# A 32x32-square transpose route through VectorE, DRAM and GpSimd in an attention-and-graph kernel

## The chip, the cores and the metric

The kernel runs on one core of one Trainium2 chip. The metric is device time in microseconds (us), lower is better. The kernel before takes 2595.5 us (median of three runs, 2594.34 to 2596.72).

## The reference

The input x has shape (16, 1024, 256): 16 batches of 1024 nodes with 256 channels. adj is 1024 x 1024. Everything is float32.

```
# layer 0, per batch
fea  = x^T                                    # (C, N)
c    = mean over channels of x                # (N,)
A    = 2*| |sigmoid(c_m - c_n) - 0.5| - 0.5 |,  symmetrised
g    = relu((fea @ (adj * A)) * para)         # (C, N)  -> queries, 4 heads of 64
k, v = x @ kv_w
out  = softmax(q k^T * scale) v               # 4 heads, concatenated to (N, C)
x1   = layernorm(x + out)
# layer 1
agg  = A_hat @ x1                             # A_hat: normalised adjacency
h    = relu(batchnorm(agg @ W1^T + b1))
y    = batchnorm(h @ W2^T + b2)
out  = layernorm(x1 + y)
```

The change touches layer 0 only, in two places: x is needed transposed (channels on partitions) for the keys and values, and the attention output, which comes out transposed (head and channel on partitions, 512 nodes along the row), has to be turned back before it is scaled by the reciprocal of the softmax denominator and added to x.

## The kernel before

Layer 0 takes the span from 0 to about 1725 us, layer 1 the rest. In layer 0 the attention of batch b and the preparation of batch b+1 are interleaved. The order on TensorE, VectorE and ScalarE is written out by hand; each of these engines executes its list in that order, so an instruction that waits holds everything behind it on its engine. SyncE (which issues most DMAs) and GpSimd also work through a list in order, but that list is put together by the scheduling layer from the program and the tile pools.

A batch has 32 *units*: 2 pairs of heads (`pr`) x 2 halves of the queries (`qh`) x 8 key blocks of 128 (`m`). A unit is

- `scores` (L926): TensorE makes 128 keys x (2 heads x 512 queries) in a PSUM tile `ps` (2 buffers),
- the exponential (L931): ScalarE, `ps` -> `p` in SBUF (pool `pp`, 4 buffers),
- `outputs` (L947): TensorE accumulates `po` over the 8 key blocks,
- `sums` (L955, L957): VectorE adds the `p` tiles up in `acc`, for the denominators. A `p` buffer is free again when both `outputs` and `sums` have read it.

Units go in bursts of two, 16 bursts (u = 0 to 15) a batch. In burst u TensorE does the scores of units 2u and 2u+1, and then the outputs of the two units before. So the exponential of the fifth unit of a batch, the first of burst u = 2, needs the `p` buffer of the first, which the VectorE addition L955 of units 0 and 1 releases.

When the 8 key blocks of one (pr, qh) are done, ScalarE (L964) and VectorE (L965) leave the unnormalised output in `oT` (128 x 512); k counts these tiles, 4 a batch, 64 in all. When both halves of a pair are done, `normalise` makes the denominators: TensorE (L977) into `den`, ScalarE (L983) to `drow`, SyncE writes 4 rows to DRAM (L985) and reads them back in columns (L990, `dcol`, 4 DMAs with 4-byte pieces).

`residual` (four times a batch) then takes VectorE's reciprocal of `dcol` (L998), 4 TensorE transposes of `oT` (L1004, `poT`), a VectorE product of `poT` with the reciprocals (L1008, `o`) and GpSimd's addition to x (L1013). All four of a batch are run in burst u = 0 of the next batch, between the projections `values` (L879) and `keys` (L866) of the batch after; these share the PSUM tiles `pt`, `ps`, `den` of the pool `t` (2 buffers). In u = 4 follow the layernorm statistics of that batch (L614, VectorE), which need all four additions, and 8 pairs of graph products (`graph_mm`, L829, first half of the channels). In u = 8 the second half of them is done, and around and between them the next-but-one batch begins: `begin` sums the channels (L774), writes the means to DRAM (L781) and reads them back on all partitions (L783, `crow`), and `transpose_x` makes 16 TensorE transposes of x (L790, `pxT`), copied to SBUF by VectorE and ScalarE (L794). `crow` is what ScalarE needs for the graph weights (`weights_abs` L810, `weights_tanh` L815; then `weights_adj` L819 on VectorE), the list `side`: 24 steps, 10 of them in bursts u = 9 to 15, the other 14 in u = 0 of the next batch.

For the first two batches the same steps run in a stretch of their own ahead of the bursts; in the last batch the residuals of batch 14 run in u = 2 and u = 5 and the first two of batch 15 in u = 13, the last two at the end.

## Time and profile before

| what | value |
|---|---|
| median of three runs | 2595.5 us |
| lowest, highest | 2594.34, 2596.72 us |
| span of the profiled execution, first to last instruction | 2592.7 us |
| TensorE busy | 2544.9 us, 98% |
| VectorE busy | 1573.9 us, 61% |
| ScalarE busy | 1214.5 us, 47% |
| GpSimd busy | 358.9 us, 14% |
| DMA | 140624 packets, 168.98 MB |
| one batch of layer 0, for example 1221.68 to 1326.09 | 104.41 us |

How to read it: the profile is one execution. The page gives its span and no other time for it; the runs' times are some us above the span. Times in timelines are us from the span's start. Busy is time in instructions, not counting the issuing of DMAs. "Idle before, releaser" is time in which an engine stood still ahead of an instruction, and what it was seen to wait for. A row of the timeline may merge several instructions in sequence (x4), and neighbouring rows overlap by some hundredths [...]. The chain of waits follows the last instruction back through what released it.

### The profile page before, as it was taken

The page shows a single profiled execution, that of the slowest core. Times are in us where ns is not written, and L with a number is a line of the kernel's source. Part 1 is how long each engine was busy: PE and PEld are TensorE (multiplying, and loading weights), DVE is VectorE, ACT ScalarE, POOL GpSimd, SP SyncE. Part 2 cuts the span into 40 slices and gives each one's busy share as a digit, 9 for nine tenths or more (in the row PEclk, how much of TensorE's full clock was granted, in tenths as well). Part 3 has the DMA queues.
Part 4 walks back from the last instruction along what each step waited for, and adds up shares of the span by engine and source line. Part 5 has one row for each costly group of instructions (what it writes and reads, how often), then busy time and mean ns, then how long its engine had stood idle before and what let it go on. Part 6 is the DMA issues. An engine that isn't in the chain of part 4 may idle for free.

```text
span 2592.7 us, 32521 instructions
## 1 busy us (share of the span) xinstructions
PE 2544.9 (98%) x13118; PEld 1119.8 (43%) x13118; DVE 1573.9 (61%) x2082; ACT 1214.5 (47%) x1499; POOL 358.9 (14%) x424
## 2 busy tenths in 40 slices
PE   9999999999999999999999999999999999999997
PEld 5443443434444444344344444344444444444455
DVE  5365655655646556566465575676556555568568
ACT  6375564655656646656466474521011100144458
POOL 0010100101101011011010110242112221010026
PEclk9999999999999999999999999999999999999999
DMA  4001101011011010110110101022122212255549
GB/s 146 1 10 42 33 10 42 2 42 34 10 42 34 9 42 1 42 33 10 42 31 12 38 5 50 10 82 92 71 86 92 97 65 98 81 195 176 189 168 345
DMA packets 140624, 168.98 MB, mean 65 GB/s; under 512 B 87089, under 2 KB 120369, under 8 KB 132017
## 3 DMA queue, kind: packets, MB, share of 16 engines
q1 hardware_dynamic: 135104, 115.95, 14.8%
q0 software_dynamic: 4832, 50.34, 4.7%
q8 instruction: 105, 1.72, 0.3%
q10 hardware_dynamic: 528, 0.52, 0.1%
q14 instruction: 55, 0.44, 0.1%
HBM read 99.36 MB, written 67.44 MB: 64 GB/s over the span
## 4 chain that ended last, share of the span: by engine, by line
PE 86%; DVE 9%; ACT 3%; issue 1%; DMA 0%; POOL 0%; SPq 0%; DVEq 0%; POOLq 0%; ACTq 0%
PE ps L926 16%; PE pg L829 16%; PE po L947 16%; PE pv L879 5%; PE b_agg L1366 4%; PE c_agg L1366 4%; PE pk L866 3%; PE po L1648 3%; PE a_agg L1366 2%; PE b_h L1398 2%; PE b_o L1574 2%; PE c_h L1398 2%; PE c_o L1574 1%; PE pxT L790 1%; PE a_h L1398 1%
## 5 line engine op out<-in xcount | busy, mean ns | idle before, releaser
L931 ACT ACTIVATE p<-ps 128x1024 f32<-128x1024 f32 x512 | 496.7, 1023 | 185.7 <-PE ps L926 156.1
L957 DVE TENSOR_TENSOR acc<-acc,p 128x1024 f32<-128x1024 f32 x384 | 485.7, 1265 | 122.8 <-ACT p L931 94.3
L926 PE MATMUL ps<-qT,kT 64*64 64x512 f32 x4096 | 491.0, 592 | 0.7 <-DVE qT L838 0.3
L947 PE MATMUL po<-p,v 64*64 64x512 f32 x4096 | 488.3, 589 | 0.8 <-ACT p L931 0.8
L829 PE MATMUL pg<-wg,x 128*128 128x512 f32 x960 | 420.9, 594 | 0.0
L1013 POOL TENSOR_TENSOR x<-x,o 128x512 f32<-128x512 f32 x64 | 122.2, 1909 | 1165.6 <-DVE o L1008 1165.6
L947 PEld LDWEIGHTS po<-p,v 64*64 64x64 f32 x4096 | 160.1, 133 | 281.0 <-issue 270.3
L829 PEld LDWEIGHTS pg<-wg,x 128*128 128x128 f32 x960 | 179.2, 190 | 221.3 <-issue 208.3
L926 PEld LDWEIGHTS ps<-qT,kT 64*64 64x64 f32 x4096 | 152.2, 133 | 281.3 <-issue 249.6
L838 DVE SCALAR_TENSOR_TENSOR qT<-pg,para_s 128x1024 f32<-128x1024 f32 (+1 forms) x34 | 39.2, 1161 | 236.1 <-PE pg L829 235.0
L819 DVE SCALAR_TENSOR_TENSOR wg<-wg,adj_s 128x1024 f32<-128x1024 f32 x128 | 162.2, 1279 | 21.7 <-ACT wg L815 21.7
L810 ACT ACTIVATE wg<-crow,ccol 128x1024 f32<-128x1024 f32 x128 | 147.1, 1150 | 8.2 <-DMA crow<-c 8.2
L815 ACT ACTIVATE wg<-wg 128x1024 f32<-128x1024 f32 x128 | 136.1, 1064 | 1.7
L879 PE MATMUL pv<-kvw_s,xT 128*128 128x256 f32 x512 | 126.8, 391 | 6.7 <-ACT kT L870 6.7
L965 DVE TENSOR_TENSOR oT<-po,oT 128x512 f32<-128x512 f32 x64 | 44.2, 691 | 145.6 <-ACT oT L964 145.6
L866 PE MATMUL pk<-xT,kvw_s 128*128 128x512 f32 x256 | 121.9, 598 | 3.3 <-ACT v L884 3.3
L624 ACT ACTIVATE x<-x,nm_l,rs_l 128x256 f32<-128x256 f32 x128 | 64.8, 588 | 110.2 <-POOL nm_l L620 110.2
L841 ACT ACTIVATE qT<-qT 128x1024 f32<-128x1024 f32 (+1 forms) x34 | 34.1, 1007 | 174.7 <-DVE qT L838 174.7
L879 PEld LDWEIGHTS pv<-kvw_s,xT 128*128 128x128 f32 x512 | 92.8, 190 | 50.1 <-ACT kT L870 25.1
L1366 PE MATMUL a_agg<-ahT,x1l 128*128 128x512 f32 x240 | 108.1, 593 | 0.7 <-ACT agg L1146 0.7
L1366 PE MATMUL b_agg<-aT,x1S 128*128 128x512 f32 x240 | 107.9, 592 | 0.0
L650 ACT COPY p_agg<-a_agg 128x512 f32<-128x512 f32 x15 | 8.8, 585 | 183.4 <-PE a_agg L1366 183.4
(204 smaller groups left out, 2933.1 us busy)
## 6 DMA issues: line engine op xcount, KB each, us to landing
h<-hw POOLq DMA_DIRECT2D x16, 2048.0 KB, 6.9
hl<-h SPq DMA_DIRECT2D x32, 1024.0 KB
x<-x POOLq DMA_DIRECT2D x16, 1024.0 KB, 4.2
x1l<-x SPq DMA_DIRECT2D x16, 1024.0 KB
xf<-x SPq DMA_DIRECT2D x16, 1024.0 KB
x<-in_x_dram SPq DMA_DIRECT2D x15, 1024.0 KB
out_dram<-o SPq DMA_DIRECT2D x12, 1024.0 KB
crow<-c SPq DMA_DIRECT2D x15, 512.0 KB
```

The lines of the kernel that those rows point to most:

```text
L810: nc.scalar.activation(w, s["crow"], AF.Abs, bias=s["ccol"][:, n : n + 1])
L815: nc.scalar.activation(w, w, AF.Tanh, scale=0.5)
L819: nc.vector.scalar_tensor_tensor(w, w, 1.0, adj_s[:, n, :], op0=ALU.subtract, op1=ALU.mult)
L829: nc.tensor.matmul(s["pg"][:, hs], xt[:, n, c * P : (c + 1) * P], s["wg", n][:, hs], start=(n == 0), stop=(n == NCH - 1),)
L866: nc.tensor.matmul(ps, kvw_s[:, c, kc * P : (kc + 1) * P], s["xT"][:, c, hs], start=(c == 0), stop=(c == CC - 1),)
L879: nc.tensor.matmul(pt[:, j * C : (j + 1) * C], s["xT"][:, c, n * P : (n + 1) * P], kvw_s[:, c, C : 2 * C], start=(c == 0), stop=(c == CC - 1),
L926: nc.tensor.matmul(ps[kh * D : (kh + 1) * D, hd * HALF : (hd + 1) * HALF], kT[r, pr, ks], qT[r, pr, qh * HALF : (qh + 1) * HALF], start=Tr ...
L931: nc.scalar.activation(p, ps, AF.Exp)
L947: nc.tensor.matmul(g["po"][kh][hd * D : (hd + 1) * D, :], s["v"][r, m, h * D : (h + 1) * D], p[r, hd * HALF : (hd + 1) * HALF], start=(m = ...
L957: nc.vector.tensor_add(g["acc"], g["acc"], p)
L1366: nc.tensor.matmul(ps, left, right, start=(start and i == 0), stop=(i == NCH // 2 - 1), skip_group_check=True,)
L1398: nc.tensor.matmul(ps, left, right, start=start, stop=True, skip_group_check=True)
```

## The change

For batches 2 to 15, x is loaded from DRAM a second time in 32x32 squares (`load_squares`: 4 DMAs of 1024 pieces of 128 bytes for each half of the channels, into a tile `xS` with one buffer), so that VectorE's transpose of 32x32 squares gives the transposed x in one instruction per half (`transpose_squares`, 128 x 1024). The first half is loaded in u = 5 of the program and transposed in u = 8, the second is loaded when the first has been transposed, and transposed in u = 11. The 16 TensorE transposes and 4 copies per batch go.

For 62 of the 64 attention outputs (all but the last pair of the last batch), `squares_to_rows` follows directly on `oT`: VectorE transposes the squares of `oT` into `oS`, SyncE writes `oS` to DRAM, and 4 SyncE DMAs of 512 pieces of 128 bytes bring it back as rows into a tile `o`, which comes from the pool `rdp` with one buffer. `residual` keeps VectorE's reciprocal; GpSimd multiplies `o` with it and adds the product to x. The TensorE transposes and VectorE's product go. The pool of `oT` has 2 buffers in place of 4.

The order of `side` changes: 10 steps in u = 0, 2 in u = 1, 2 in u = 2.

```diff
+    o_d = [
+        dram.tile([NQ, SQ, HALF // SQ, SQ], F32, tag=f"o_{g}", name=f"o_{g}")
+        for g in range(2 * B * H // 2)
+    ]
...
-        tc.tile_pool(name="op", bufs=4) as op,
+        tc.tile_pool(name="op", bufs=2) as op,
+        tc.tile_pool(name="xsp", bufs=1) as xsp,
...
+        def load_squares(b, c):
+            xs = st[b]["xS", c] = xsp.tile([P, N // SQ, SQ], F32, tag="xS", name=f"xS_{b}_{c}")
+            src = x[b].rearrange("(j k) (c q i) -> c q k j i", k=SQ, q=NQ, i=SQ)
+            for q in range(NQ):
+                nc.sync.dma_start(xs[q * SQ : (q + 1) * SQ], src[c, q])
...
+            def transpose_squares(c):
+                if c == 0:
+                    s["xT"] = xTp.tile([P, CC, N], F32, tag="xT", name=f"xT_{b}")
+                nc.vector.transpose(
+                    s["xT"][:, c, :], s["xS", c].rearrange("p j i -> p (j i)")
+                )
+                if c == 0:
+                    load_squares(b, 1)
...
-            for i in range(2 * CC):
-                first.append((transpose_x, (i // 2, i % 2) if b else (i % 2, i // 2)))
+            if b < 2:
+                for i in range(2 * CC):
+                    first.append((transpose_x, (i // 2, i % 2) if b else (i % 2, i // 2)))
+            else:
+                first += [(transpose_squares, (c,)) for c in range(CC)]
...
                 nc.vector.tensor_add(g["oT"], g["po"][1], g["oT"])
+                if (b, pr) != (B - 1, PAIRS - 1):
+                    squares_to_rows(b, pr, qh)
...
+        def squares_to_rows(b, pr, qh):
+            g = G[b, pr, qh]
+            k = (b * PAIRS + pr) * 2 + qh
+            oS = op.tile([P, HALF], F32, tag="oS", name=f"oS_{k}")
+            nc.vector.transpose(oS, g["oT"])
+            nc.sync.dma_start(o_d[k].rearrange("q i j d -> (q i) (j d)"), oS)
+            g["o"] = rdp.tile([P, 4, NQ, SQ], F32, tag="o", name=f"o_{k}")
+            src = o_d[k].rearrange("q i (n m) d -> m i n q d", m=NQ)
+            for m in range(NQ):
+                nc.sync.dma_start(g["o"][m * SQ : (m + 1) * SQ], src[m])
...
             nc.vector.reciprocal(r_all[:, k], g["col"])
-            if (b, pr) == (B - 1, PAIRS - 1):
-                pt = tile_s(f"poT_{k}")[:, H0]
-            else:
-                pt = tile_t(f"poT_{k}")
+            r = r_all[:, k].unsqueeze(3).to_broadcast([P, 4, 2, D])
+            xs = s["x"][:, 4 * qh : 4 * qh + 4, pr * P : (pr + 1) * P]
+            if (b, pr) != (B - 1, PAIRS - 1):
+                o = g["o"].rearrange("p n q d -> p n (q d)")
+                oh = o.rearrange("p n (h d) -> p n h d", d=D)
+                nc.gpsimd.tensor_tensor(oh, oh, r, ALU.mult)
+                nc.gpsimd.tensor_tensor(xs, xs, o, ALU.add)
+                return
...
                 if u == 5 and b + 2 < B:
                     load_x(b + 2)
+                    load_squares(b + 2, 0)
...
                         if b:
                             run(steps, 1)
-                            run(side, 2)
+                            if i < 5:
+                                run(side, 2)
...
-                    run(side, 99)
                     run(full, 1)
+                elif u < 4:
+                    run(side, 2 if u < 3 else 99)
...
                 elif u == 8:
-                    run(next_first, 3)
-                    for n in range(NCH):
-                        run(steps, 1)
-                        if n == 3:
-                            run(next_first, 2)
+                    run(next_first, 2)
+                    run(steps, NCH)
                     run(sums, 1)
                 elif u > 8:
+                    if u == 11:
+                        run(next_first, 1)
                     run(next_side, 2 - u % 2)
```

More of the change, by code (lines that the diff above doesn't have):

```diff
@@ L573, in fast_path @@
     h_d = [dram.tile([P, HC, N], F32, tag=f"h_{b}", name=f"h_{b}") for b in range(B)]
+    SQ = 32
+    NQ = P // SQ
+    o_d = [
+        dram.tile([NQ, SQ, HALF // SQ, SQ], F32, tag=f"o_{g}", name=f"o_{g}")
+        for g in range(2 * B * H // 2)
+    ]
     ident = const.tile([P, P], F32, name="ident")
@@ L998, in residual @@
             nc.vector.reciprocal(r_all[:, k], g["col"])
-            if (b, pr) == (B - 1, PAIRS - 1):
-                pt = tile_s(f"poT_{k}")[:, H0]
-            else:
-                pt = tile_t(f"poT_{k}")
+            r = r_all[:, k].unsqueeze(3).to_broadcast([P, 4, 2, D])
[6 more added lines that the diff above has]
+                return
+            pt = tile_s(f"poT_{k}")[:, H0]
             for j in range(4):
@@ L1008, in residual @@
             nc.vector.tensor_mul(
-                o, pt.rearrange("p (n h d) -> p n h d", h=2, d=D),
-                r_all[:, k].unsqueeze(3).to_broadcast([P, 4, 2, D]),
+                o, pt.rearrange("p (n h d) -> p n h d", h=2, d=D), r
             )
-            xs = s["x"][:, 4 * qh : 4 * qh + 4, pr * P : (pr + 1) * P]
             nc.gpsimd.tensor_tensor(xs, xs, o.rearrange("p n h d -> p n (h d)"), ALU.add)
```

## The prediction

> **What bounds the kernel now.** First the page's busy times and its chain of waits:

> ```profile
> PE 2544.9 (98%) x13118; PEld 1119.8 (43%) x13118; DVE 1573.9 (61%) x2082; ACT 1214.5 (47%) x1499; POOL 358.9 (14%) x424
> ...
> PE 86%; DVE 9%; ACT 3%; issue 1%; DMA 0%; POOL 0%; SPq 0%; DVEq 0%; POOLq 0%; ACTq 0%
> ```

> TensorE (PE) works almost without a gap, and the chain is PE's: whatever leaves PE shortens the kernel, as long as nothing else makes PE wait. Next, busy times by stretch for one batch (sum 104.41 us; PE, PEld, DVE, ACT, POOL, clock, DMA share):

> ```profile
> 1221.68:1326.09 104.41, 103.70 (x677) 44.12 (x679) 61.94 (x74) 60.64 (x73) 10.82 (x10) 1.00 0.10 26
> ```

> The neighbouring batches read the same within 0.1 us. PE is the only full engine; VectorE (DVE) has 42 us free per batch and DMA nine tenths. Third, the groups of instructions that the change removes:

> ```profile
> L1004 PE MATMUL poT<-ident,oT 128*128 128x128 f32 x256 | 37.9, 273 | 0.0
> ...
> L790 PE MATMUL pxT<-ident,x 128*128 128x128 f32 x256 | 36.3, 286 | 6.3 <-DMA x<-in_x_dram 5.1 <-DVE xT L794 1.0 <-ACT kT L870 0.2
> ...
> L1008 DVE TENSOR_TENSOR o<-poT,r_all 128x512 f32<-128x512 f32 x64 | 44.3, 691 | 60.4 <-PE poT L1004 38.6 <-POOL x L1013 19.8
> ```

> Busy over count is 0.148 and 0.142 us of PE per transpose. Last, timelines around the batch boundary (start, us, engine), of SyncE's issues, GpSimd, VectorE and ScalarE:

> ```profile
> 1278.08 0.34 SPq L783 DMA_DIRECT2D crow<-c  x1
> ...
> 1284.82 2.03 SPq L990 DMA_DIRECT2D dcol<-den  x4
> 1315.10 1.12 SPq L985 DMA_DIRECT2D den<-drow  x4
> 1316.32 2.26 SPq L990 DMA_DIRECT2D dcol<-den  x4
> ```
> ```profile
> 1317.19 2.17 POOL L1013 TENSOR_TENSOR x<-x,o 128x512 f32<-128x512 f32 x1 [68.30 <-DVE o L1008]
> 1320.16 1.27 POOL L1013 TENSOR_TENSOR x<-x,o 128x512 f32<-128x512 f32 x1 [0.80 <-DVE o L1008]
> ```
> ```profile
> 1314.21 0.20 DVE L998 RECIPROCAL r_all<-dcol 128x8 f32<-128x8 f32 x1
> ...
> 1328.41 1.22 DVE L955 TENSOR_TENSOR acc<-p,p 128x1024 f32<-128x1024 f32 x1
> ```
> ```profile
> 1330.61 1.94 ACT L931 ACTIVATE p<-ps 128x1024 f32<-128x1024 f32 x2 [1.50 <-PE ps L926]
> ```

> The reader sees: the denominators are read back (1316.32) well before the third reciprocal at 1323.04, so no reciprocal waits. The L955 addition at 1328.41 frees the `p` buffers for the exponentials at 1330.61, just in time. Take note of this place.

> [...] No row here is a VectorE transpose. [...] GpSimd [...] 2.17 us beside the L819 instructions, 1.27 us alone. [...] the `dcol` reads[...] load the engines by 0.3 to 0.8 each.

> **What goes.** At the boundary PE runs from 1309.31 (first `values`) to 1326.02 (scores of u = 1), 16.71 us. By successive starts the four `values`, three `keys` and the denominator product need 1.83+1.81+0.99+1.83+1.82+1.83+1.72+1.83 = 13.66; four `poT` and their gaps are 3.05. In u = 8 two groups of `pxT` take 1.04 each, 2.08. There are 14 such boundaries (u = 0 of batches 1 to 14, transposed x of batches 2 to 15): 14 x 5.13 = 71.8 us. In the last batch 6 residuals x 4 x 0.148 = 3.6. Together **-75.4 us**. Also off: 62 VectorE products and 28 VectorE copies (62 us), 28 ScalarE copies (16 us), all beside PE.

> **What comes, hidden.** VectorE: 62 transposes of 512 and 28 of 1024 per row. At [...] L794 (0.69 us for 512) [...] I take 0.8 and 1.6, 94 us against 62 removed, in its free 42 us a batch. GpSimd: 62 products, 1.27 to 2.17 us, in an engine 86% idle. DMA packets: 28 x 4096 + 62 x 2048 = 241,664 of 128 bytes. The `dcol` reads cost 8.4 ns of an engine per 4-byte packet (17.2 us of engine time by quarter-microsecond windows, 2048 packets); the x load at 1252.64 moves 1 KB packets at about 46 ns. Between these, 13 ns: 197 us of 16 engines, 8% of the span. The squares of x are in time: the first half is fetched a batch ahead; the second has from u = 8 to u = 11 (over 13 us) for 4 x 1024 packets (about 7 us at the `dcol` pace). The four `side` steps that move fall into u = 1 and 2, where the graph products are still two bursts away.

> **What comes, in the way.** All `o` share one buffer, so four outputs pass through it in turn at the boundary, and SyncE's list as built for the changed kernel is: first row of `den`; the 4 reads of the second `o` (wait for GpSimd to finish the first); rows 2 to 4 of `den`; one `dcol` read; the 4 reads of the third `o` (wait for the second); **then the other three `dcol` reads**, then the fourth `o`. VectorE's third and fourth reciprocal need those, and behind them on VectorE stands the L955 addition that frees the `p` buffers. On the timeline's clock:
> - first reciprocal done 1314.6 (1314.41, and 0.2 for the added transpose);
> - GpSimd: [...] product beside L819 2.17, addition 1.28 and gaps: 1318.3;
> - SyncE reads the second `o`: four `dcol` reads take 1.03 us to the first data and 0.69 each; I take 1.0 + 4 x 0.8 + 0.2 = 4.4 from 1318.45: 1322.85;
> - GpSimd again, product 1.7 (between 1.27 and 2.17), addition 1.28, hops: 1326.1;
> - third `o` and three `dcol` reads from 1326.25: 1.0 + 4 x 0.8 + 3 x 0.69 + 0.3: 1332.8;
> - fourth reciprocal 1333.15, L955 addition 1334.4, exponential done 1335.6, PE's scores of u = 3 start 1335.7.

> Without that, PE would be there at 1322.97 (start of u = 1) + 4 x 1.72 + 0.1 = 1329.95. The stall is **5.75 us** per boundary, against 5.13 saved. Bounds: with `dcol`'s own pace, lone products and free transposes 3.55; with 128-byte packets at the 46 ns of the 1 KB ones (1.5 us per 512) 11. The statistics in u = 4 come after the fourth addition (1344), where 14 us of graph products cover them. A second wait: PE now reaches u = 9 2.08 us earlier, while `crow` is 0.8 us later (transpose ahead of the sums); it landed at 1283.1 by the DMA windows, 2.2 before its use at 1285.30. It is about 1.0 late, ScalarE's exponentials have 0.8 in hand before PE needs them: 0.3 us (0 to 2). In the last batch all `dcol` reads stand ahead of the `o` reads: no stall.

> **Sum.** 14 x (5.75 + 0.3) - 75.4 = +9.3 us on the profiled execution's 2592.7 us span. The page gives no other time for it; the runs' median lies 2.8 above the span, which I carry over: 2595.5 + 9.3 = 2605.

> **The rivals.** (a) *Faster: the landings are quick.* Stall 3.55: 14 x (3.55 + 0.3) - 75.4 = -21.5, 2574. For: `dcol` shows that pace. Against: its packets are 32 times smaller. It decides once the stall is under 4.7 us at `crow`'s 0.3; with no stall at all 2520. (b) *Packets of 128 bytes cost as much as 1 KB ones*: stall 11, 14 x 11.3 - 75.4 = +83, 2678. [...] Against: 46 ns is what 1 KB takes. (c) *`crow` bounds as well*: x squares share queue and engines with it, 2 us per batch: 2629. (d) *PE's transposes were hidden and nothing is won*: their idle column shows 0.0 and PE has no gaps, so I give this nothing.

> **How the numbers follow.** Likeliest case 0.50 (2590 to 2635 by itself), (a) 0.27, (b) 0.12, (c) 0.11. 0.2% is 5.2 us, about what a measurement here can tell. Faster: 0.25 of (a) and 0.03 of the likeliest, 0.28. Same: 0.02 and 0.11, 0.13. Slower: 0.36, (b), (c): 0.59. The range goes from (a) with some more luck to (b): 2565 to 2680.

> **What would show it.** Right: VectorE idle at its third and fourth reciprocal for some 10 us per boundary, released by the DMA of `dcol`; SyncE waiting for GpSimd ahead of the `o` reads; PE idle before the scores, released by ScalarE, some 80 us in all; per batch about 105 us. Wrong: PE without gaps at u = 3 and batches near 99.3 us (the chain is shorter), or gaps at u = 9 or u = 11 (`crow`, `xS`), or `o` reads far from 4.4 us.

## The result and the profile after

The changed kernel takes 2633.65 us (median of four runs, 2627.43 to 2635.44) against 2595.58 for the kernel before on the same chip: ratio 1.0144, 95% interval 1.0129 to 1.0158, so 38 us slower. Its profiled execution took 2633.63 us, span 2631.9, which is 39.2 above the span before. Line numbers below are those of the changed kernel (in the lines shown of kernels with more `o` buffers they are 2 to 7 higher): scores L951, exponential L956, `outputs` L972, the first sum L980 and the later ones L982, `oS` transpose L1002, its write L1003, the `o` reads L1007, `den` rows L1024, `dcol` L1029, reciprocal L1037, GpSimd's product L1043 and addition L1044, x squares L761, their transpose L812, write of the means L794, `crow` L796, graph weights L832, graph products L851.

From the page of the changed kernel, the busy times, the chain of waits and the costliest matmul (busy us, mean ns of one | idle us before it), and then the same matmul from the page of the kernel before:

```profile
PE 2525.3 (96%) x12646; PEld 1071.5 (41%) x12646; DVE 1616.8 (61%) x2082; ACT 1200.2 (46%) x1471; POOL 437.5 (17%) x486
...
issue 36%; PE 35%; DVE 17%; POOL 4%; DMA 3%; SPq 3%; ACT 1%; POOLq 0%; DVEq 0%; ACTq 0%
...
L951 PE MATMUL ps<-qT,kT 64*64 64x512 f32 x4096 | 516.2, 618 | 69.7 <-ACT p L956 68.3
```
```profile
L926 PE MATMUL ps<-qT,kT 64*64 64x512 f32 x4096 | 491.0, 592 | 0.7 <-DVE qT L838 0.3
```

TensorE's busy time fell by 20 us and its list by 472 instructions, but its share fell from 98% to 96%. VectorE's share of the chain rose from 9% to 17%, and GpSimd, DMA and SyncE's queue have entered it; the 36% under "issue" is time for which the profile shows no wait, so the chain's shares don't price the stall. The matmul's line holds two losses: 68 us of waiting for the exponentials, and a mean of 618 ns where the same matmul took 592 before. The mean granted TensorE clock is 0.983 (before 0.998).

The waits of the changed kernel (us in total, times, longest) say which instruction is late:

```profile
DVE r_all L1037 <- DMA dcol<-den: 147.5, 28, 10.3
...
POOL o L1043 <- DMA o<-o: 118.7, 24, 6.2
...
ACT p L956 <- DVE acc L980: 81.1, 16, 6.1
PE ps L951 <- ACT p L956: 68.3, 21, 5.2
...
ACT wg L832 <- DMA crow<-c: 25.9, 15, 8.3
```

It is the forecast chain: VectorE waits for `dcol`, GpSimd for `o`, ScalarE for VectorE's sum, TensorE for ScalarE. The last row is a second, smaller wait, for `crow`. The timelines of one batch boundary (start, us) give the order. SyncE first, then GpSimd:

```profile
1236.10 0.25 SPq L1024 DMA_DIRECT2D den<-drow  x1
1238.80 2.61 SPq L1007 DMA_DIRECT2D o<-o  x4
1241.45 1.05 SPq L1024 DMA_DIRECT2D den<-drow  x3
1242.55 0.39 SPq L1029 DMA_DIRECT2D dcol<-den  x1
1247.09 2.61 SPq L1007 DMA_DIRECT2D o<-o  x4
1249.74 1.73 SPq L1029 DMA_DIRECT2D dcol<-den  x3
```
```profile
1235.53 1.04 POOL L1043 TENSOR_TENSOR o<-o,r_all 128x512 f32<-128x512 f32 x1 [62.00 <-DVE r_all L1037]
1236.64 2.13 POOL L1044 TENSOR_TENSOR x<-x,o 128x512 f32<-128x512 f32 x1
1244.68 1.04 POOL L1043 TENSOR_TENSOR o<-o,r_all 128x512 f32<-128x512 f32 x1 [5.90 <-DMA o<-o]
1245.80 1.26 POOL L1044 TENSOR_TENSOR x<-x,o 128x512 f32<-128x512 f32 x1
```

SyncE issues `o` reads only when GpSimd's addition of the round before has ended (1238.77, 1247.06), and three small `dcol` reads stand behind them. Then VectorE, ScalarE and TensorE:

```profile
1252.17 0.20 DVE L1037 RECIPROCAL r_all<-dcol 128x8 f32<-128x8 f32 x1 [9.93 <-DMA dcol<-den]
1253.31 0.20 DVE L1037 RECIPROCAL r_all<-dcol 128x8 f32<-128x8 f32 x1 [0.93 <-DMA dcol<-den]
1253.43 1.20 DVE L980 TENSOR_TENSOR acc<-p,p 128x1024 f32<-128x1024 f32 x1
```
```profile
1254.72 1.94 ACT L956 ACTIVATE p<-ps 128x1024 f32<-128x1024 f32 x2 [5.64 <-DVE acc L980]
```
```profile
1249.07 1.90 PE L972 MATMUL po<-p,v 64*64 64x512 f32 x16
1255.80 3.29 PE L951 MATMUL ps<-qT,kT 64*64 64x512 f32 x16 [4.84 <-ACT p L956]
1258.92 1.89 PE L972 MATMUL po<-p,v 64*64 64x512 f32 x16
```

The middle row carries something that nobody forecast: after the hole, scores that take 1.90 to 2.00 us elsewhere in this timeline take 3.29. SyncE's and VectorE's rows show what a wait does to the list behind it: the three `dcol` reads start at 1249.74, when the `o` reads ahead of them have been issued (1247.09 and 2.61), and the first sum at 1253.43, after waits of 9.93 and 0.93 us at the two reciprocals.

Cutting every batch at the starts of TensorE's rows gives a ledger by stage. Each figure is the mean over the 13 full periods of one trace, in us:

| kernel | u=0: projections | u=1 to graph | graph, u=4 to 7 | u=8 | u=9 to 15 | period |
|---|---|---|---|---|---|---|
| before | 16.71 | 13.89 | 29.54 | 16.63 | 27.63 | 104.41 |
| after | 13.56 | 20.76 | 29.54 | 14.93 | 28.32 | 107.10 |
| x squares only | 16.71 | 13.89 | 29.54 | 14.93 | 28.07 | 103.14 |
| output squares only | 13.56 | 20.22 | 29.54 | 16.63 | 27.63 | 107.58 |
| two `o` buffers | 13.56 | 17.40 | 29.54 | 14.93 | 28.58 | 104.01 |
| three `o` buffers | 13.56 | 14.39 | 29.54 | 14.93 | 28.66 | 101.08 |
| `o` reads on GpSimd | 13.56 | 13.89 | 30.43 | 14.93 | 28.41 | 101.22 |
| three buffers, early means | 13.56 | 14.49 | 29.54 | 14.93 | 27.63 | 100.15 |
| GpSimd reads, early means | 13.56 | 13.89 | 30.18 | 14.93 | 27.63 | 100.19 |
| all three | 13.56 | 13.89 | 29.54 | 14.93 | 27.63 | 99.55 |
| hole filled, 5 matmuls | 13.56 | 19.09 | 29.54 | 14.93 | 28.28 | 105.39 |
| hole filled, 2 matmuls | 13.56 | 19.41 | 29.55 | 14.93 | 28.29 | 105.74 |

For the changed kernel: 3.15 and 1.70 us saved in u=0 and u=8, 6.87 lost ahead of the graph products, 0.69 in u=9 to 15. Over 13 periods that is 35.0 of the 39.2 us of span; what lies before the first boundary is 1.9 shorter (the first of the 14 savings in u=8 is in it), and what follows the start of layer 1, its first `pagg` matmul, is 6.2 longer (901.1 for 894.9).

### The profile page after: what moved, and what is told of

Its sections match the earlier page's. It is cut to its first block, busy times and chain, and to the rows that moved or that the text cites. A ratio compares the mean times of both kernels' runs of the same rounds, so it can differ in the third digit from the quotient of the medians.

```text
span 2631.9 us, 32424 instructions
## 1 busy us (share of the span) xinstructions
PE 2525.3 (96%) x12646; PEld 1071.5 (41%) x12646; DVE 1616.8 (61%) x2082; ACT 1200.2 (46%) x1471; POOL 437.5 (17%) x486
## 2 busy tenths in 40 slices
DMA packets 396979, 216.19 MB, mean 82 GB/s; under 512 B 335504, under 2 KB 368784, under 8 KB 388368
## 3 DMA queue, kind: packets, MB, share of 16 engines
q1 hardware_dynamic: 391456, 163.16, 24.5%
## 4 chain that ended last, share of the span: by engine, by line
issue 36%; PE 35%; DVE 17%; POOL 4%; DMA 3%; SPq 3%; ACT 1%; POOLq 0%; DVEq 0%; ACTq 0%
DVE acc L982 4%; PE b_agg L1410 4%; PE c_agg L1410 4%; PE po L1692 3%; PE ps L951 2%; PE a_agg L1410 2%; SPq L1007 2%; PE b_h L1442 2%; PE po L972 2%; PE pg L851 2%; PE b_o L1618 2%; POOL x L1044 2%; DMA o<-o 2%; PE c_h L1442 2%; PE c_o L1618 1%
## 5 line engine op out<-in xcount | busy, mean ns | idle before, releaser
L956 ACT ACTIVATE p<-ps 128x1024 f32<-128x1024 f32 x512 | 498.6, 1022 | 249.4 <-PE ps L951 132.0
L982 DVE TENSOR_TENSOR acc<-acc,p 128x1024 f32<-128x1024 f32 x384 | 507.5, 1322 | 126.7 <-ACT p L956 98.1
L951 PE MATMUL ps<-qT,kT 64*64 64x512 f32 x4096 | 516.2, 618 | 69.7 <-ACT p L956 68.3
L972 PE MATMUL po<-p,v 64*64 64x512 f32 x4096 | 496.0, 597 | 0.0
L851 PE MATMUL pg<-wg,x 128*128 128x512 f32 x960 | 420.0, 595 | 0.0
L951 PEld LDWEIGHTS ps<-qT,kT 64*64 64x64 f32 x4096 | 149.4, 136 | 378.7 <-issue 202.5
L972 PEld LDWEIGHTS po<-p,v 64*64 64x64 f32 x4096 | 163.8, 136 | 292.8 <-issue 281.7
L1043 POOL TENSOR_TENSOR o<-o,r_all 128x512 f32<-128x512 f32 x62 | 79.1, 1275 | 1221.1 <-DVE r_all L1037 1063.1
L851 PEld LDWEIGHTS pg<-wg,x 128*128 128x128 f32 x960 | 179.9, 190 | 239.6 <-issue 220.1
L860 DVE SCALAR_TENSOR_TENSOR qT<-pg,para_s 128x1024 f32<-128x1024 f32 (+1 forms) x34 | 39.2, 1161 | 228.3 <-PE pg L851 227.4
L841 DVE SCALAR_TENSOR_TENSOR wg<-wg,adj_s 128x1024 f32<-128x1024 f32 x128 | 164.6, 1306 | 18.6 <-ACT wg L837 18.6
L832 ACT ACTIVATE wg<-crow,ccol 128x1024 f32<-128x1024 f32 x128 | 146.6, 1146 | 25.9 <-DMA crow<-c 25.9
L1044 POOL TENSOR_TENSOR x<-x,o 128x512 f32<-128x512 f32 x62 | 118.7, 1914 | 4.9
L990 DVE TENSOR_TENSOR oT<-po,oT 128x512 f32<-128x512 f32 x64 | 44.1, 689 | 96.6 <-ACT oT L989 96.6
```

The costliest lines, as they stand in the source:

```text
L832: nc.scalar.activation(w, s["crow"], AF.Abs, bias=s["ccol"][:, n : n + 1])
L841: nc.vector.scalar_tensor_tensor(w, w, 1.0, adj_s[:, n, :], op0=ALU.subtract, op1=ALU.mult)
L851: nc.tensor.matmul(s["pg"][:, hs], xt[:, n, c * P : (c + 1) * P], s["wg", n][:, hs], start=(n == 0), stop=(n == NCH - 1),)
L951: nc.tensor.matmul(ps[kh * D : (kh + 1) * D, hd * HALF : (hd + 1) * HALF], kT[r, pr, ks], qT[r, pr, qh * HALF : (qh + 1) * HALF], start=Tr ...
L956: nc.scalar.activation(p, ps, AF.Exp)
L972: nc.tensor.matmul(g["po"][kh][hd * D : (hd + 1) * D, :], s["v"][r, m, h * D : (h + 1) * D], p[r, hd * HALF : (hd + 1) * HALF], start=(m = ...
```

## The experiments

Theory 1: the stall comes from the place of the `dcol` reads in SyncE's list, behind `o` reads that wait for GpSimd because there is one `o` buffer. Theory 2: it is the work itself, the 128-byte packets, GpSimd's products beside VectorE or VectorE's transposes. Theory 3: the late `crow` costs most. Results are medians of four runs (twelve for two buffers); the ratio is to the kernel before.

**Three buffers for `o`.** The room comes from `oT` and `oS`, which get one buffer each; the last pair's two `oT` lie in the `xS` buffer.

```diff
-        tc.tile_pool(name="op", bufs=2) as op,
+        tc.tile_pool(name="op", bufs=1) as op,
+        tc.tile_pool(name="osp", bufs=1) as osp,
+        tc.tile_pool(name="rop", bufs=3) as rop,
...
-            g["o"] = rdp.tile([P, 4, NQ, SQ], F32, tag="o", name=f"o_{k}")
+            g["o"] = rop.tile([P, 4, NQ, SQ], F32, tag="o", name=f"o_{k}")
```

> The change with three buffers for o in place of one (the room for it taken from oT and oS, one buffer each). SyncE's list then has the reads of the third o ahead of the den rows, or waiting for GpSimd's first sum alone, and all four dcol loads directly after the den rows. Theory 1 (the stall after u=0 comes from SyncE's order: dcol behind reads that wait for GpSimd): the idle of TensorE ahead of the second score unit of u=0's follower, about 4.8 us in each of 14 batches, goes, and with it the slow score and output units that follow it (1.3 to 2.4 us); the granted clock returns to about 0.998; 2530 to 2560 us, median guess 2545. Theory 2 (128-byte packets, or GpSimd's products beside VectorE, or VectorE's transposes, cost it): the packets and all GpSimd and VectorE work are the same, so 2620 to 2640. Theory 3 (the late crow after the x squares costs most of it): also about 2620 to 2640, with the wait for crow unchanged.

Measured: 2548.9 us, ratio 0.9824 (0.9808 to 0.9841), clock 0.996. All work and all packets of the change are there (396,978, one fewer than after), and the kernel is 85 us faster than after. Theories 2 and 3 fall for the main effect. The timeline of SyncE at the same boundary shows the order turned round:

```profile
1178.52 2.60 SPq L1014 DMA_DIRECT2D o<-o  x4
1181.17 1.06 SPq L1031 DMA_DIRECT2D den<-drow  x3
1182.28 2.75 SPq L1036 DMA_DIRECT2D dcol<-den  x4
```

Half a microsecond per batch is left: one round of `o` reads still stands ahead of the `den` rows, VectorE waits 3.8 us for the reciprocal, works off its list late, and TensorE waits a little at the graph products. From the timelines of VectorE and TensorE:

```profile
1185.77 0.20 DVE L1044 RECIPROCAL r_all<-dcol 128x8 f32<-128x8 f32 x1 [3.81 <-DMA dcol<-den]
```
```profile
1198.03 14.00 PE L853 MATMUL pg<-wg,x 128*128 128x512 f32 x32 [0.48 <-ACT p L958]
```

**The `o` reads on GpSimd's queue**, with one buffer as in the change.

```diff
-                nc.sync.dma_start(g["o"][m * SQ : (m + 1) * SQ], src[m])
+                nc.gpsimd.dma_start(g["o"][m * SQ : (m + 1) * SQ], src[m])
```

> The change with one buffer for o still, but with the four reads of each o issued from GpSimd's queue in place of SyncE's. SyncE's list then has den rows and all four dcol in a row. Theory 1 (the wait stands in SyncE's order and not in the buffer): the third and fourth reciprocals are early, the stall goes although each o still waits for the one before; 2535 to 2575 us. A form of theory 1 in which the one buffer itself is what is late (statistics of x1 wait for the fourth o): a new wait at the statistics, 2580 to 2630. Theory 2 (packets, GpSimd, VectorE) and theory 3 (crow): 2620 to 2640.

Measured: 2547.01 us, ratio 0.9814 (0.9797 to 0.983). One word in the code takes the loss away: the buffer is as scarce as before, but nothing small waits behind it, and the stage ahead of the graph is back at 13.89. From its timelines, SyncE and then GpSimd at a batch boundary:

```profile
1276.81 1.13 SPq L1024 DMA_DIRECT2D den<-drow  x4
1278.04 2.03 SPq L1029 DMA_DIRECT2D dcol<-den  x4
```
```profile
1279.79 2.92 POOL L1007 DMA_DIRECT2D o<-o  x4 [0.29 <-POOL x L1044]
1285.87 1.04 POOL L1043 TENSOR_TENSOR o<-o,r_all 128x512 f32<-128x512 f32 x1 [3.16 <-DMA o<-o]
...
1289.45 2.90 POOL L1007 DMA_DIRECT2D o<-o  x4 [0.29 <-POOL x L1044]
1294.19 1.68 POOL L1043 TENSOR_TENSOR o<-o,r_all 128x512 f32<-128x512 f32 x1 [1.85 <-DMA o<-o]
```

All four `dcol` reads are issued ahead of the second round. The rounds themselves are no quicker: from the first issue to the product they take 5.3 us on average over 46 rounds of this trace, and 5.2 in the changed kernel. So faster reads are not what took the stall away. So the place in SyncE's list is the cause, and the single buffer alone is not. What the buffer still costs shows elsewhere, in the waits of this kernel: the statistics wait for the fourth addition, and the stage of the graph products goes from 29.54 to 30.43.

```profile
DVE st_l L620 <- POOL x L1044: 43.4, 15, 4.2
```

These transfers also changed in kind: the trace counts 273,970 packets in place of 396,979, so this run alone says nothing on the price of 128-byte packets; three buffers does.

**Squares for x only**, the outputs by TensorE and VectorE as before (the residual's old lines and the four `oT` buffers are back as well).

```diff
-                if (b, pr) != (B - 1, PAIRS - 1):
-                    squares_to_rows(b, pr, qh)
```

> Only the squares for x; attention outputs go back to TensorE's transposes and VectorE's product. Theory 1: no stall after u=0 beyond that of the kernel before; TensorE is freed of the four pxT per batch (1.7 to 2.1 us) and pays for the later crow (about 1 us per batch): 13 such batches, so 2580 to 2600 us, about the kernel before. Theory 3 (crow is the main cost): 2615 or more. Theory 2 in its form that blames the packets of x: 2610 or more.

Measured: 2578.77 us, ratio 0.9932 (0.9915 to 0.9949); just under the forecast band. This half of the change is a gain of 16 us: 14 x (1.70 - 0.44) = 17.6 by the ledger. The 0.44 in u=9 to 15 is its own cost, as that stage stands at 27.63 without it.

**Squares for the outputs only**, x by TensorE as before (with the old order of steps in u=8).

```diff
-            if b < 2:
+            if True:
                 for i in range(2 * CC):
                     first.append((transpose_x, (i // 2, i % 2) if b else (i % 2, i // 2)))
```

> Only the squares for the attention outputs; x is transposed by TensorE. Theory 1: the stall after u=0 is all here, 14 x (6.4 - 3.15) - 3.6 us = +42: about 2637 us, with the granted clock at 0.98. Theory 3 (crow): the loss is gone, 2560 or less. Theory 2 in its form that blames the packets of o: 2625 to 2640 as well; the first two kernels tell it from theory 1.

Measured: 2638.27 us, ratio 1.0167 (1.015 to 1.0184), clock 0.982. The whole loss is here: 14 x (6.33 - 3.15) = 44.5 us by the ledger, 43 in the times. `crow` plays no part in it.

**Two buffers for `o`**: as three, with `bufs=2`.

> As the kernel with three buffers for o, with two. By SyncE's order the den rows 2 to 4 and the four dcol now stand behind the reads of the third o, which wait for GpSimd's sum on the first o; one round of GpSimd and read fewer than with one buffer, one more than with three. Theory 1 (order of SyncE behind the o buffers): dcol of the third reciprocal lands about 1250 where it was 1253 in the profile after, so the idle of about 5 us per batch shrinks to about 2 us, and with a shorter idle the slow matmuls after it shrink as well: 2565 to 2595 us. A rival that takes the three buffers' gain to come from the layout alone (oT and oS in one buffer each, second x squares later): as with three buffers, 2545 to 2552.

Measured: 2590.23 us, ratio 0.9983 (0.9974 to 0.9992). One, two and three buffers give 6.87, 3.51 and 0.50 us of loss in the stage ahead of the graph: each further buffer, that is one round of GpSimd and reads less for `dcol` to wait for, takes 3.0 to 3.4 us out of that stage. (What is lost is not of one kind: with one buffer 2.1 us of it are slow matmuls, see the filled hole below; with two, 1.4 are a wait of TensorE at the graph products.) Two and three buffers have the same layout otherwise, so the layout is not the reason.

**Early means, with three buffers**, and the same with one buffer and GpSimd's reads.

```diff
                 elif u == 8:
-                    run(next_first, 2)
+                    run(next_first, 1)
...
+                elif u == 7:
+                    run(next_first, 1)
```

> Three buffers for o, and the means of x (csum, ccol, ncol, the write of c and its read as crow) one stage earlier, at u=7 instead of u=8, so that c is written about 4 us sooner. Theory of the lost microsecond in u=9 to 15 (ScalarE waits for crow, 1.6 us behind two exponentials, and TensorE waits for those): the wait of L834 for crow goes, the stage returns from 28.6 to 27.6 us per batch: 2549 less 13 to 14 x 1.0 = about 2535 us, 2530 to 2540. A rival (that microsecond comes from the second x transpose on VectorE, 1.24 us at u=11, and not from crow): no change, 2545 to 2552.

> One buffer for o with its reads on GpSimd's queue, and the means of x at u=7 instead of u=8. Same theories as with three buffers: crow to blame, 2547 less 13 to 14 x 1.0 = about 2533 us, 2528 to 2540; second x transpose to blame, 2543 to 2551. Whichever of the two is lower is the best version that these reasons point to.

Measured: 2536.53 us, ratio 0.9771 (0.9754 to 0.9787), and 2535.72, ratio 0.9769 (0.9753 to 0.9785). In both the stage u=9 to 15 is at 27.63 in every batch, while the second transpose of x on VectorE is still in it, so it was `crow`. In the changed kernel, the timelines of SyncE and ScalarE show its path:

```profile
1298.36 0.36 SPq L794 DMA_DIRECT2D c<-ncol  x1
...
1309.77 0.33 SPq L796 DMA_DIRECT2D crow<-c  x1
```
```profile
1314.01 1.15 ACT L832 ACTIVATE wg<-crow,ccol 128x1024 f32<-128x1024 f32 x1 [1.63 <-DMA crow<-c]
```

The read `crow` waits for the 4 KB write of the means, here for 11.4 us from issue to issue. The write did not become slower with the change; from SyncE's timeline of the kernel before:

```profile
1060.16 0.36 SPq L781 DMA_DIRECT2D c<-ncol  x1
1071.45 0.34 SPq L783 DMA_DIRECT2D crow<-c  x1
```

Over the 13 periods this time goes from 9.1 to 11.9 us before and from 8.8 to 11.5 after, with means of 10.25 and 10.15. What changed is the start: `c` is issued 12.70 us ahead of the first scores of u=9 before, and 10.28 after, because TensorE is there 1.70 sooner and the write comes 0.72 later. So the long ones now bind: in the six periods with 9.6 us or less the stage u=9 to 15 takes 28.0 on average, in the seven with 10.5 or more 28.6. Early means begin that wait one burst sooner; from SyncE's timeline with three buffers, where the graph weights come at 1236.79 without a wait:

```profile
1216.48 0.36 SPq L796 DMA_DIRECT2D c<-ncol  x1
1227.67 0.34 SPq L798 DMA_DIRECT2D crow<-c  x1
```

**Filling the hole.** The changed kernel with matmuls that nobody reads, put where TensorE would wait; five of them, and in a second kernel two (`range(2)`).

```diff
+                if u == 3 and 0 < b < B:
+                    pf = tile_t(f"fill_{b}")
+                    for f in range(5):
+                        nc.tensor.matmul(
+                            pf, adj_s[:, f % NCH, :P], adj_s[:, f % NCH, H0],
+                            start=True, stop=True,
+                        )
```

> The change as it is, with five matmuls that nobody reads (adjacency by adjacency, 0.875 us each, 4.4 us in all) put ahead of the scores of u=3 in batches 1 to 14, where TensorE otherwise waits about 4.8 us: extra work, in the hole only. The stall's other cost is unchanged. Theory A (matmuls after the hole are slow because TensorE was idle): the stretch after the hole falls from 3.3 to 3.7 us to 1.9 us, the granted clock returns to 0.99 or more, and the kernel gets faster by doing more: 14 x 1.3 to 1.9, 2607 to 2616 us. Theory B (they are slow from something beside them, such as transfers or VectorE at that time): 2630 to 2640.

> The change as it is, with two unread matmuls (1.75 us) in the hole where five were before, so that about 3.1 us of idle are left just ahead of the scores of u=3. If the slow matmuls after the hole come from an idle of about 4 to 5 us and not from a shorter one, most of what five matmuls brought is there with two: 2608 to 2620 us, first stretch after the hole 1.9 to 2.5 us in most batches. If any idle slows them in proportion, two fifths of the gain: about 2624 us. If the fill helped for another reason (only as long as it reaches up to the scores), 2630 to 2638.

Measured: 2611.33 us with five, ratio 1.0067 (1.005 to 1.0084), clock 0.996; 2610.17 with two, ratio 1.0052 (1.0035 to 1.0069), clock 0.99. The kernel with more work is 22 us faster than the changed kernel. From the timelines of TensorE, five and then two matmuls:

```profile
708.39 1.95 PE L951 MATMUL ps<-qT,kT 64*64 64x512 f32 x16
```
```profile
922.70 1.98 PE L1261 MATMUL fill<-adj_s 128*128 128x512 f32 x4
926.31 2.00 PE L951 MATMUL ps<-qT,kT 64*64 64x512 f32 x16 [1.62 <-ACT p L956]
...
1340.08 1.98 PE L1261 MATMUL fill<-adj_s 128*128 128x512 f32 x4
1345.09 3.69 PE L951 MATMUL ps<-qT,kT 64*64 64x512 f32 x16 [3.03 <-ACT p L956]
1348.56 3.14 PE L972 MATMUL po<-p,v 64*64 64x512 f32 x16
```

With the hole filled the scores after it take 1.95, where they take 3.17 to 3.69 in the changed kernel, so theory A holds: TensorE was slow because it had been idle. The granted clock says the same. In the changed kernel's trace it stands at one half for 3.41 or 6.83 us around the first scores after the hole at each of the 14 boundaries, and with five matmuls nowhere in layer 0. Three stretches of the changed kernel around the hole shown above (busy PE, PEld, DVE, ACT, POOL, then clock, DMA share, GB/s):

```profile
1251.00:1255.10 4.10, 0.00 (x0) 0.00 (x0) 1.89 (x4) 0.38 (x1) 2.51 (x2) 1.00 0.21 5
1255.20:1258.50 3.30, 2.70 (x16) 0.88 (x20) 3.20 (x3) 2.11 (x3) 0.56 (x1) 0.50 0.25 40
1258.60:1262.00 3.40, 3.40 (x40) 1.11 (x36) 3.30 (x4) 1.36 (x3) 1.65 (x1) 1.00 0.24 38
```

What the stall and the slow clock cost apart is read from the starts of TensorE's rows, as means over the 13 periods. In the changed kernel the scores of u=3 start 11.71 us after those of u=1, for 6.92 before: a hole of 4.79. From there to the graph products it takes 9.05, for 6.98: 2.07 of slow matmuls. Filling the hole won 1.67 of these 2.07 (19.09 for 20.76 in the ledger), because five matmuls take 4.5 us themselves and end as late as the exponentials come, or later, in 10 of 14 boundaries, and because the graph products then wait 0.23 on average.

With two matmuls 1.62 to 3.20 us of idle are left, and the outcome varies with it: the first scores take 2.00 in six of the 14 boundaries and 2.64 to 3.69 in eight, where 2.5 or less had been expected in most. As this fill never delays the scores, the kernel gains nearly the same all the same; so the fill need not reach up to them.

**All three repairs**: three buffers, reads on GpSimd's queue, early means.

> All three repairs in one kernel: three buffers for o, its reads on GpSimd's queue, means at u=7. The two earlier combinations each keep a loss in one stage per batch: three buffers with SyncE's reads 0.60 us ahead of the graph (14.49 for 13.89), one buffer with GpSimd's reads 0.64 us in the stage of the statistics (30.18 for 29.54). Theory 1: the first is the late dcol behind SyncE's reads, the second the fourth o that waits for its buffer; together both go, the period is 13.56 + 13.89 + 29.54 + 14.93 + 27.63 = 99.55 us, 14 x 0.6 = 8 us below the 2536 of each: 2526 to 2531. A rival (both come from GpSimd's and VectorE's additions slowing each other, wherever the reads are): 2533 to 2539.

Measured: 2524.85 us (2524.6 to 2526.21), ratio 0.973 (0.9713 to 0.9746), 70 us faster than the kernel before and the fastest here; just below the forecast band. From its page:

```profile
PE 2485.0 (98%) x12646; PEld 1067.9 (42%) x12646; DVE 1666.0 (66%) x2082; ACT 1196.4 (47%) x1471; POOL 600.5 (24%) x734
```

TensorE is at 98% again, now of a shorter span. The ledger's three stages outside the savings equal those before, and every period reads 99.54 or 99.55. So the two residues were what they were taken for, and the rival falls: additions that take longer beside VectorE (in the changed kernel's timeline 2.13 us beside L841, 1.26 with VectorE idle) cost nothing that TensorE sees. Both savings together, 4.85 us, come through whole.

## Why the prediction was right, and where its sizes were off

The forecast was slower, 2605 in 2565 to 2680; 2633.65 was measured. The mechanism is the one written down, step by step: one `o` buffer, SyncE's list, late `dcol`, two reciprocals ahead of L980, no free `p`, TensorE waiting at u = 3. TensorE waited for ScalarE for 68.3 us in all (some 80 forecast), and a batch took 107.10 us (about 105). The time lies at the upper edge of the likeliest case (2590 to 2635), but it got there by terms that the sum did not have, so the size is no success of the working. The direction does not hang on them: with the hole filled the kernel is still 16 us slower than before.

By span the sum missed 30 us (39.2 for 9.3). The first five terms below, in their order, make -1 + 5 - 13 + 29 + 5 of it over 14 batches, layer 1 makes 6, and the start and the last batch -1. By terms, per batch:

- **Savings at the boundary**: 3.05 forecast, 3.15 measured.
- **Savings in u=8**: 2.08 forecast, 1.70 measured, 5 us in all. This term was mis-sized: it added the busy times of two `pxT` groups, 1.04 each. Matmul rows overlap; by successive starts, as used for the other saving, the trace before gives 0.93 (1265.05 to 1265.98) and 0.87 (1272.85 to 1273.72).
- **The stall**: 5.75 forecast, 4.79 measured. Errors of single steps cancelled in part, which is luck. GpSimd's product took 1.04 in both rounds, for 2.17 and 1.7, and its addition 2.13 in the first, for 1.28. The second and third `o` read took 5.5 on average (at the boundary shown the second took 5.9, 1238.80 to 1244.68), for 4.4; reads far from 4.4 were one of the prediction's own signs of being wrong. From the third `o` read to the last reciprocal 6.4, for 6.9.
- **What the stall does to TensorE**: no term for it in the sum; 2.07 per batch, 29 us over 14 boundaries. This is the step that failed: the working let TensorE go on after the hole as if nothing had been.
- **`crow`**: 0.3 forecast, 0.69 measured, 5 us in all. The shift was seen: 2.88 us (2.08 + 0.8) for the 2.42 measured. What failed is the slack: it was read at one boundary, where the write of the means took 9.1 us, and in other periods of the same kernel it takes up to 11.9. (By the prediction's own figures the landing is 2.88 - 2.2 = 0.7 late, not 1.0.)
- **Hidden work**: right. VectorE's transposes took 711 and 1238 ns, for 512 and 1024 a row; the 0.8 and 1.6 us taken were the author's estimate, which no trace had shown. Together with the packets and GpSimd's products they cost nothing once the order is mended: in the last kernel only the two savings are left in the ledger.
- **Last batch**: 3.6 forecast. From its last boundary to layer 1 the changed kernel takes 179.6 us against 179.7, although that boundary by itself loses 5.1 (22.20 ahead of the graph for 13.89, 1.4 above the mean, less the 3.15 saved); so 5.2 are saved behind it.
- **Layer 1**: no term; 6.2 us longer. About 3 of it lie at its start, where TensorE idles 1.91 us ahead of `a_agg` (0.68 before) and the first group then takes 5.37 in place of 3.70. Some 2 more go with a second stretch at half clock, 6.83 us from 2538.55, after a pause of 2.98 ahead of `pf`; the kernel before has the same pause and no slow clock there (see the last section). The rest, after TensorE's last row, was not followed up, and in other kernels here layer 1 differs by 0.8 to 5.4 us from the kernel before.

Of the rivals, quick landings (2574) did not come: an `o` read took 5.5, more than the working had, where this rival took `dcol`'s pace for 128-byte pieces. But products even quicker than its lone ones did come, so that the stall of 4.79 ended near the 4.7 under which it was to decide. Packets at the price of 1 KB ones failed as well: queue 1 carries 256,352 packets more than before, and its share of 16 engines' span rose from 14.8 to 24.5%, about 16 ns for each, the larger `oS` packets included, where 13 was taken and 46 feared. `crow` did bind, at a third of that rival's price, and in addition to the stall.

## What to carry to other kernels

Before a DMA is put on a queue that works in order, as SyncE's did here, ask what it waits for and what small thing stands behind it; moving 248 reads to another queue was worth 87 us, and a round of them took about as long as before. When a change frees the bounding engine, look for the shortest wait that it newly meets, cost the order of each queue round by round, and add what a pause does to TensorE's next matmuls (2.07 us a batch here, after a hole of 4.79). A change that loses by one wait may hold a gain: each half was worth measuring alone.

## What the runs showed of the hardware that was not expected

The traces also show what goes with it in between. Their stretches at half clock in layer 0 last 3.41 us or twice that, and within one trace they start whole multiples of 3.413 us apart (in the changed kernel, for example, at 1040.10, 1149.33 and 1255.14, which are 32 and 31 such steps). Cutting each trace on this grid, all 40 slow rows had at least 1.96 us of their pause inside one interval, and 14 of the 15 others at most 1.88 (the last one 1.99). In layer 1 the `a_agg` group above was slow after 1.91, all in one interval, and the pause of 2.98 ahead of `pf` falls 1.49 and 1.49 into two intervals in the kernel before, and 2.16 and 0.83 in the changed one, where it was slow. So in these traces the slow rows went with what of a pause fell into one interval, and pauses of nearly the same length cost differently: after those of 1.96 to 2.23 us the scores took from 2.00 to 3.32, after those of 1.47 to 1.89 about 2.00.

One 4 KB write in 4-byte pieces held the DMA that waits for it for 8.7 to 12.4 us in all 180 cases of the twelve traces, the kernel before among them, after an issue of 0.36. In the kernel before, the 1 MB load of x issued at 1252.64 was through by 1257.60 (the DMA share was 0.05 in the fifth of a microsecond before that and 0.00 after it), so in these runs the bytes of a transfer did not tell when the next could start.
